# Two transformer layers on one core: when row maxima are turned, where counts run, and where scratch lies in the operand stage

## The chip, the cores and the metric

The kernel runs as one program on one core of a Trainium2 chip. Time is the device time of one execution in microseconds (us). TensorE (PE) does the matmuls and transposes, VectorE (DVE), ScalarE (ACT) and GpSimd (POOL) do the rest, and SyncE (SP) issues most DMAs. Each engine works through its own queue in order; semaphores order the engines among each other. PE writes its results to PSUM, which POOL does not touch in this kernel; everything else lies in SBUF.

## The reference

`x` is 2048 tokens by 512 features in float32. Each layer adds two branches to `x`, both computed from the same layer norm `xn`.

```
xn = layernorm(x)
x  = x + linear_attention(xn) + routed_experts(xn)        # layer 0
xn = layernorm(x)
x  = x + L1_attn(xn) + L1_ffn(xn)                         # layer 1

L1_attn: q, k, v = split(xn @ w_qkv)       # 16 heads of 32
         q, k = rope(rmsnorm(q)), rope(rmsnorm(k))
         softmax(q k^T / sqrt(32)) over the 1024 tokens before each token, and itself
         out = (p @ v) @ w_out
L1_ffn:  scores = xn @ w_router; take the 256 tokens of the highest score, sorted by place
         a transformer block on these 256 tokens alone: 16 heads of 128, 8 key heads,
         rms norms, rope by place, causal softmax, gated MLP of width 2048
         the result goes back to those 256 rows, the other rows keep xn
```

## The kernel before, in words

The span has four stages: layer 0, then for layer 1 the operand stage, the FFN block and attention. The change touches the operand stage and the FFN block.

**Operand stage.** The loop over 16 token tiles of 128 (`NT`, `t`) makes the queries, keys and values of layer 1. `turned` loads a tile of `xn` and transposes it on PE (`tr`, L100); ACT copies the result to `xnt`. Three groups of four matmuls (`p`, L782, 128x512 each) follow for q, k and v. `normed_qk` squares q and k on ACT (`t1`, L641), takes the norm on DVE (`rr`, `qk`, L642 to L645) and applies the rope on POOL (L650 to L660), for the last tile on DVE. One tile later `turned_qk` transposes q and k on PE (`trqk`); ACT copies to `qT`, DVE to `kT`.

**Row maxima.** Attention later needs the maximum of each score row. `maxima(i, ...)` finds it for query tile `i` in *steps*: four score matmuls (`pa`, L515, one for each head of a group, each listed as two records), mask matmuls (L521, L523), then one DVE reduction (`mx`, L527) of the whole PSUM buffer. There is one such buffer of four banks (`ps_a`, `bufs=1`), so a step's matmuls wait for the reduction of the step before. After a tile's last step DVE makes `nm` and `parts` (L531 to L534), PE transposes `parts` (`tn`, L537) and ACT copies to `negT`. All of it is issued at once, so `tn` stands on PE's queue right behind the last step.

**Steps between other work.** `Steps.some` spends a rate: at each call it owes a share of a step and issues one when a whole one is owed, of tiles below a bound only. In the operand stage the rate is 0.85, with six calls per tile, for query tiles 0 to 9 (`EARLY`); `early.upto(EARLY)` issues what is left before the last `turned_qk`. Tiles 10 to 15 are a second `Steps` object, `late`, with a PSUM pool of its own in the FFN block and a rate of 0.38; `late.upto(NT)` closes it. A query tile has four to twelve steps, 144 in all.

**Routing.** `routing` is a generator; each `next(route)` (four per tile) issues one piece. The first four pieces transpose the score row to all partitions (`srow`, L698, copied by ACT). Then each of the 16 token tiles has two count pieces on DVE: how many scores are larger (L713, L718, whole rows) and how ties are broken (L725, L726). From the counts come the places (`pplace`, `pos`), which POOL uses to scatter token numbers to lists in DRAM (L753), to load them back and to gather the 256 rows (`xs`, L579).

**FFN block.** It begins with a norm and transposes of the gathered rows (`hn_a`, L838, `trh_a`, L841) and the first projection (`k2p`, L852), whose weights are loaded by SP (`k2w`). `late.some` is called between its matmuls.

**What sets the order.** The order of the code is not the order on the engines: a planner reorders the instructions of each engine by their dependencies, and the engine then works in that order. In the profile counts ran far ahead of the token tile in whose pieces they were written: all sixteen lie between 782 and 862 us. Buffers are tiles of pools, and a pool's buffer that is reused, or lies where a closed pool's buffers lay, waits for those.

Of the kernel before, what the change touches and what calls it, by code (L numbers as in the profile page):

```python
# [19 lines left out]
P = 128  # L20
T = 2048
# [17 lines left out]
def two_layer_kernel(ctx: ExitStack, tc: tile.TileContext, a: dict, out: bass.AP):  # L39
# [452 lines left out]
    parts = []  # L492
    for n in range(2):
        pn = const([P, NC, 4, HD], f"parts{n}", l1, BF16)
        G.memset(pn, 0.0)
        parts.append(pn)

    def maxima(i, wk, ps_a, ps_t, ttag):
# [5 lines left out]
        mx = wk.tile([P, NC, 4, 3], F32, tag="mx", name=f"mx_{i}")  # L504
# [25 lines left out]
        nm = wk.tile([P, NC, 4], F32, tag="nm", name=f"nm_{i}")  # L530
        V.tensor_reduce(nm, mx[:, :, :, :nch], AX.X, ALU.max, negate=True)  # L531
        pn = parts[i % 2]
        vcopy(pn[:, :, :, 0], nm)
        V.tensor_tensor(pn[:, :, :, 1], nm, pn[:, :, :, 0], ALU.subtract)  # L534
        tn = ps_t.tile([P, NC, P], BF16, tag=ttag, name=f"tn_{i}")
        for g in range(NC):
            PE.transpose(tn[:, g, :], pn[:, g].rearrange("p h d -> p (h d)"), ident_b)  # L537
        scopy(negT[:, :, i * P : (i + 1) * P], tn)

    class Steps:  # L540


        def __init__(self, tiles, rate, **kw):
            self.tiles, self.kw = list(tiles), kw
            self.steps, self.now, self.rate, self.owed = iter(()), -1, rate, 0.0
            self.busy = False
# [10 lines left out]
        def one(self, below=NT):  # L557
            while self.now < below:
                if next(self.steps, False) is not False:
                    return True  # L560
                self.busy = False
                if not self.tiles or self.tiles[0] >= below:
                    return False
                self.now, self.busy = self.tiles.pop(0), True
                self.steps = maxima(self.now, **self.kw)
            return False

        def left(self):
            return self.tiles or self.busy

        def upto(self, below):
            while self.one(below):
                pass

# [7 lines left out]
    EARLY = 10  # L582


    with ExitStack() as p4:
        w4 = p4.enter_context(tc.tile_pool(name="w4", bufs=1, side="right", reuse_waits="tile"))
        xq = p4.enter_context(tc.tile_pool(name="xq", bufs=3, side="right", reuse_waits="tile"))
        r5 = p4.enter_context(tc.tile_pool(name="r5", bufs=1, side="right", reuse_waits="tile"))
        wk = p4.enter_context(tc.tile_pool(name="wk4", bufs=2, side="right", reuse_waits="tile"))
        ps_a = p4.enter_context(tc.tile_pool(name="ps_a4", bufs=1, **tight))  # L590
# [35 lines left out]
        def turned(t):  # L626
# [4 lines left out]
            xnt = wk.tile([P, NC, P], F32, tag="xnt", name=f"xnt_{t}")  # L631
# [3 lines left out]
        def normed_qk(t, pp):  # L635

            qk = wk.tile([P, 2, HEADS, HD], F32, tag="qk", name=f"qk_{t}")
            t1 = wk.tile([P, 2, HEADS, HD], F32, tag="t1", name=f"t1_{t}", bufs=1)
            rr = wk.tile([P, 2, HEADS], F32, tag="rr", name=f"rr_{t}")
# [13 lines left out]
            t2 = wk.tile([P, 2, HEADS, HD], F32, tag="t2", name=f"t2_{t}", bufs=1)  # L653
# [16 lines left out]
        def routing():  # L670
# [22 lines left out]
            srow = const([P, T], "srow", r5)  # L693
# [15 lines left out]
            for t in range(NT):  # L709
                own = score[:, t : t + 1]  # L710
                j1 = wk.tile([P, T], F32, tag="j1", name=f"j1_{t}", bufs=1)
# [37 lines left out]
            for n in range(4):  # L749
                place = wk.tile([P, 2 * HEADS], mybir.dt.int32, tag="rr", name=f"place_{n}")  # L750
# [23 lines left out]
        early = Steps(range(EARLY), 0.85, wk=wk, ps_a=ps_a, ps_t=ps_t, ttag="tr")  # L774
        xnt, last_qk = turned(0), None
        for t in range(NT):
            pp = []
            for j in range(3):
                pj = ps.tile([P, D], F32, tag="pj", name=f"p{j}_{t}")
                for c in range(NC):  # L780
                    w = w_v[:, c, :] if j == 2 else w_qk[:, c, j * D : (j + 1) * D]
                    PE.matmul(pj, xnt[:, c, :], w, start=c == 0, stop=c == NC - 1)  # L782
                    if c == 1:
                        early.some(min(t if j == 2 else t - 1, EARLY))
                        next(route, None)
                pp.append(pj)
                if j < 2 and last_qk is not None:
                    turned_qk(t - 1, last_qk, j)
                if j == 2 and t < NT - 1:
                    xnt = turned(t + 1)  # L790
                early.some(min(t if j else t - 1, EARLY))
                if j == 1:
# [513 lines left out]
```

## Time and profile before

| | us |
|---|---|
| median of 3 runs | 1873.57 |
| lowest, highest | 1873.55, 1880.08 |
| profiled execution | 1869.43 |
| its span | 1867.7 |
| layer 0 | 0 to 762.7 |
| operand stage | 762.7 to 1150.7 (388.0) |
| FFN block | 1150.7 to 1462.9 (312.2) |
| attention | 1462.9 to 1867.7 (404.8) |

The stages are cut at PE's first matmul of each. The granted clock, a share of PE's full speed, is 0.97 over the whole span. The token tiles of the operand stage start, by their first transpose, at 762.7, 783.4, 806.2, 831.3, 859.4, 878.9, 898.6, 915.9, 936.6, 961.8, 982.3, 1005.4, 1037.8, 1059.6, 1080.2 and 1102.1; the last one's window runs to the first `k2p` at 1150.7.

A group of instructions is written as line, engine, operation and `output<-input`, with buffer numbers left out. A wait is written `A <- B`: A's engine was idle before A, and B's end released it. Idle time of an engine that is not the bottleneck costs nothing by itself.

### The profile page before, as it was taken

Reading aid. Unit: us, or ns where it says so; the run is one execution under the profiler, and the core shown is the slowest. Engines: PE = TensorE matmul, PEld = TensorE weight load, DVE = VectorE, ACT = ScalarE, POOL = GpSimd, SP = SyncE. Lnnn points to the kernel's source line nnn. Section 1 sums busy time; section 2 is a strip of 40 time slices with the busy share of each in tenths; the row PEclk is TensorE's granted clock in tenths of the full one; section 3 lists DMA queues with packets and bytes.
Section 4 is the critical chain, followed back from the end, with each engine's and each line's share of the span. In section 5 each row is a group of like instructions: output and inputs, shape, how many; then the busy total and the mean of one; then the engine's idle time right before and its main releaser. Section 6 shows DMA issues by size and latency. Waiting matters only on the chain. (4 is left out here: it accounts for less than half of the span.)

```text
span 1867.7 us, 20604 instructions
## 1 busy us (share of the span) xinstructions
PE 1740.5 (93%) x8120; PEld 767.4 (41%) x8120; DVE 1008.1 (54%) x1445; ACT 573.7 (31%) x923; POOL 497.2 (27%) x372
## 2 busy tenths in 40 slices
PE   7999999999999999868988887999999999999999
PEld 4555444344444333323433333454565333333333
DVE  6775645436445343696666564575555455444344
ACT  3212334233233243111111111142100366446463
POOL 2110000100100110333344431331000467458583
PEclk9999999999999999989999897999999899999999
DMA  9301001210213130100001004311132300110100
GB/s 362 128 29 43 23 28 39 85 34 29 72 53 74 33 109 23 62 23 23 23 23 29 26 12 149 122 51 68 46 111 92 91 1 1 35 57 1 46 1 35
DMA packets 61810, 107.12 MB, mean 57 GB/s; under 512 B 12209, under 2 KB 13745, under 8 KB 61201
## 3 DMA queue, kind: packets, MB, share of 16 engines
q1 hardware_dynamic: 55280, 104.01, 16.7%
q0 software_dynamic: 1152, 1.21, 0.4%
q8 instruction: 63, 1.03, 0.2%
q10 hardware_dynamic: 5280, 0.59, 0.2%
q14 instruction: 35, 0.28, 0.0%
HBM read 84.14 MB, written 21.65 MB: 57 GB/s over the span
## 5 line engine op out<-in xcount | busy, mean ns | idle before, releaser
L527 DVE TENSOR_REDUCE mx<-pa 128x4 f32<-128x1536 f32 (+3 forms) x144 | 252.9, 1756 | 178.2 <-PE pa L523 83.8
L1210 POOL TENSOR_TENSOR acc<-acc,pt 128x1024 f32<-128x1024 f32 (+3 forms) x126 | 253.8, 2047 | 122.1 <-ACT pt L1137 75.8
L1137 ACT ACTIVATE pt<-ps 128x1024 f32<-128x1024 f32 (+3 forms) x208 | 182.2, 923 | 138.1 <-DVE ps L1128 86.4
L515 PE MATMUL pa<-kT,qT 32*128 32x384 f32 (+3 forms) x1152 | 158.0, 562 | 47.5 <-DVE mx L527 39.3
L1104 PE MATMUL ps<-qT,kT 32*128 32x512 f32 (+3 forms) x1152 | 162.0, 535 | 8.6 <-ACT pt L1137 8.1
L93 POOL TENSOR_TENSOR xr<-xr,xn 128x512 f32<-128x512 f32 x16 | 27.0, 1697 | 493.6 <-DVE xn L87 493.6
L424 PE MATMUL acc<-h,rw2T 128*128 128x512 f32 x256 | 135.3, 616 | 14.9 <-DVE h L290 14.3
L288 ACT ACTIVATE r_e<-eg 128x512 f32<-128x512 f32 x128 | 75.8, 594 | 222.4 <-PE eg L419 202.4
L782 PE MATMUL p<-w_qk,xnt 128*128 128x512 f32 x256 | 129.7, 631 | 8.3 <-ACT xnt L107 8.3
L290 DVE TENSOR_TENSOR h<-ea,r_e 128x512 f32<-128x512 f32 x128 | 87.0, 686 | 87.2 <-ACT r_e L289 59.9
L421 PE MATMUL ea<-xw,rw1T 128*128 128x512 f32 x256 | 130.7, 592 | 0.0
L419 PE MATMUL eg<-xl,rwgT 128*128 128x512 f32 x256 | 130.7, 592 | 0.0
L1128 DVE TENSOR_TENSOR ps<-ps,maskT 128x256 f32<-128x256 f32 (+1 forms) x144 | 68.3, 514 | 100.3 <-PE ps L1111 97.2
L1104 PEld LDWEIGHTS ps<-qT,kT 32*128 32x128 f32 x1152 | 62.2, 186 | 116.5 <-issue 55.4
L515 PEld LDWEIGHTS pa<-kT,qT 32*128 32x128 f32 x1152 | 52.0, 191 | 138.3 <-DVE mx L527 88.0
L1177 PE MATMUL av<-pt,v 128*32 128x512 f32 (+3 forms) x1024 | 102.3, 485 | 0.2
L415 DVE TENSOR_TENSOR xw<-xw,xl 128x512 f32<-128x512 f32 x64 | 43.9, 685 | 94.9 <-DMA xw<-w_d 94.9
L1219 DVE RECIPROCAL sm<-sm 128x128 f32<-128x128 f32 x64 | 61.8, 965 | 57.4 <-PE sm L1191 56.0
L424 PEld LDWEIGHTS acc<-h,rw2T 128*128 128x128 f32 x256 | 43.4, 188 | 95.5 <-DVE h L290 79.4
L289 ACT ACTIVATE r_e<-r_e 128x512 f32<-128x512 f32 x128 | 80.2, 629 | 6.4 <-issue 1.9
L650 POOL TENSOR_TENSOR t<-qk,cosg 128x1024 f32<-128x1024 f32 x15 | 35.3, 2354 | 161.7 <-DVE qk L645 145.5
L421 PEld LDWEIGHTS ea<-xw,rw1T 128*128 128x128 f32 x256 | 48.6, 190 | 61.2 <-issue 60.8
(278 smaller groups left out, 2542.2 us busy)
## 6 DMA issues: line engine op xcount, KB each, us to landing
xw<-w_d SPq DMA_DIRECT2D x64, 256.0 KB, 3.2
x<-in_x SPq DMA_DIRECT2D x16, 256.0 KB, 4.3
res_d<-x SPq DMA_DIRECT2D x16, 256.0 KB, 2.3
xr<-res_d SPq DMA_DIRECT2D x16, 256.0 KB, 4.8
xn_d<-xn SPq DMA_DIRECT2D x16, 256.0 KB, 2.4
res_d<-xr SPq DMA_DIRECT2D x16, 256.0 KB, 2.0
xnq<-xn_d SPq DMA_DIRECT2D x16, 256.0 KB, 2.9
v_d<-vt SPq DMA_DIRECT2D x16, 256.0 KB, 2.9
```

Of the source, the lines that this page charges most:

```text
L289: S.activation(r, r, AF.Square)
L290: V.tensor_tensor(dst, pa, r, ALU.mult)
L419: PE.matmul(pg, rwgT[:, e, hb], xl, start=True, stop=True)
L421: PE.matmul(pa, rw1T[:, e, hb], xw, start=True, stop=True)
L424: PE.matmul(acc, rw2T[:, j, e, :], h, start=e == 0 and j == 0, stop=e == E - 1 and j == 1,)
L515: PE.matmul(pS[:, h, : w * P], qT[r, g, i * P : (i + 1) * P], kT[r, g, ks], start=True, stop=not (edge or last),)
L527: V.tensor_reduce(mx[:, g, :, c], pS[:, :, : w * P], AX.X, ALU.max)
L782: PE.matmul(pj, xnt[:, c, :], w, start=c == 0, stop=c == NC - 1)
L1104: PE.matmul(pS[h // 2][:, h % 2, t0 * P - q0 : (t1 + 1) * P - q0], kT[r, g, kb * P : (kb + 1) * P], qT[r, g, t0 * P : (t1 + 1) * P], start ...
L1137: S.activation(pT[:, :, :n], pS[hp][:, :, :n], AF.Exp)
L1177: PE.matmul(self.av[h * HD : (h + 1) * HD, t0 * P - o : (t1 + 1) * P - o], vs[kb // 4][:, kb % 4, hs], got[h // 2][:, h % 2, t0 * P - q0 : ...
L1210: eng.tensor_tensor(part, part, got[hp][:, :, : q1 - q0], ALU.add)
```

## The change

The turn of a tile's maxima (`tn` and its copy) is no longer part of the tile's last step: `maxima` hands it out, and `Steps.one` issues it after the next step's matmuls. `mx` and `nm` become pairs of fixed buffers. `early` and `late` become one object with one PSUM pool over both stages; the limit `EARLY` goes, so in the operand stage steps of any finished tile are issued at rate 0.85 and no block of steps is issued at its end but three single ones around the last two `turned_qk`. What is left goes to the FFN block at a rate worked out from the number left over 190.

In the loop, the next tile's `xn` is transposed after the first of the three matmul groups rather than the third, and the previous tile's q and k after the second and third rather than the first and second. Some steps are allowed one call later (bound `t - 1` within the groups, `t` only at the third one's end). The routing starts at token tile 1. Each pair of counts first copies its two score columns into a buffer that rotates with `xnt`, so that it can't be issued far ahead of its tile. Scratch pools are split: `t1`, `rr`, `t2` and `place` lie in a pool `wka`, `srow` and `j1` in a pool `r6`, so that other buffers than before lie over those of layer 0.

The diff, without its empty lines:

```diff
@@ -489,19 +489,21 @@
-    parts = []
+    parts, mxs, nms = [], [], []
     for n in range(2):
         pn = const([P, NC, 4, HD], f"parts{n}", l1, BF16)
         G.memset(pn, 0.0)
         parts.append(pn)
-    def maxima(i, wk, ps_a, ps_t, ttag):
+        mxs.append(const([P, NC, 4, 3], f"mx{n}", l1))
+        nms.append(const([P, NC, 4], f"nm{n}", l1))
+    def maxima(i, ps_a):
         nb = min(i + 1, NWB)
         kb0 = i + 1 - nb
         nch = -(-nb // 4)
-        mx = wk.tile([P, NC, 4, 3], F32, tag="mx", name=f"mx_{i}")
+        mx, nm, pn = mxs[i % 2], nms[i % 2], parts[i % 2]
         for g in range(NC):
             lo = 0
             for c in range(nch):
@@ -527,23 +529,29 @@
                 V.tensor_reduce(mx[:, g, :, c], pS[:, :, : w * P], AX.X, ALU.max)
                 yield
                 lo += w
-        nm = wk.tile([P, NC, 4], F32, tag="nm", name=f"nm_{i}")
         V.tensor_reduce(nm, mx[:, :, :, :nch], AX.X, ALU.max, negate=True)
-        pn = parts[i % 2]
         vcopy(pn[:, :, :, 0], nm)
         V.tensor_tensor(pn[:, :, :, 1], nm, pn[:, :, :, 0], ALU.subtract)
-        tn = ps_t.tile([P, NC, P], BF16, tag=ttag, name=f"tn_{i}")
-        for g in range(NC):
-            PE.transpose(tn[:, g, :], pn[:, g].rearrange("p h d -> p (h d)"), ident_b)
-        scopy(negT[:, :, i * P : (i + 1) * P], tn)
+        def turn(pool, tag):
+            tn = pool.tile([P, NC, P], BF16, tag=tag, name=f"tn_{i}")
+            for g in range(NC):
+                PE.transpose(tn[:, g, :], pn[:, g].rearrange("p h d -> p (h d)"), ident_b)
+            scopy(negT[:, :, i * P : (i + 1) * P], tn)
+        yield turn
     class Steps:
-        def __init__(self, tiles, rate, **kw):
-            self.tiles, self.kw = list(tiles), kw
-            self.steps, self.now, self.rate, self.owed = iter(()), -1, rate, 0.0
-            self.busy = False
+        def __init__(self, ps_a):
+            self.ps_a, self.pool, self.tag, self.rate = ps_a, None, None, 0.0
+            self.steps, self.now, self.owed, self.done, self.turn = iter(()), -1, 0.0, 0, None
+        def place(self, pool, tag, rate):
+            self.pool, self.tag, self.rate = pool, tag, rate
         def some(self, below=NT, weight=1.0):
@@ -556,21 +564,30 @@
         def one(self, below=NT):
             while self.now < below:
-                if next(self.steps, False) is not False:
+                step = next(self.steps, False)
+                if step is None:
+                    self.done += 1
+                    self.turned()
                     return True
-                self.busy = False
-                if not self.tiles or self.tiles[0] >= below:
+                if step is not False:
+                    self.turned()
+                    self.turn = step
+                elif self.now + 1 >= below:
                     return False
-                self.now, self.busy = self.tiles.pop(0), True
-                self.steps = maxima(self.now, **self.kw)
+                else:
+                    self.now += 1
+                    self.steps = maxima(self.now, self.ps_a)
             return False
-        def left(self):
-            return self.tiles or self.busy
-        def upto(self, below):
-            while self.one(below):
+        def turned(self):
+            if self.turn is not None:
+                self.turn(self.pool, self.tag)
+                self.turn = None
+        def rest(self):
+            while self.one():
                 pass
+            self.turned()
     def rows_of(j):
         return bass.IndirectOffsetOnAxis(ap=idx[:, j : j + 1], axis=0)
@@ -579,15 +596,20 @@
         G.indirect_dma_start(out=dst, out_offset=None, in_=src[:, :], in_offset=rows_of(j))
     tight = dict(space=PSUM, reuse_waits="tile")
-    EARLY = 10
+    NSTEPS = sum(NC * -(-min(i + 1, NWB) // 4) for i in range(NT))
+    pa_in = ExitStack()
+    ps_a = pa_in.enter_context(tc.tile_pool(name="ps_a", bufs=1, **tight))
+    early = Steps(ps_a)
     with ExitStack() as p4:
         w4 = p4.enter_context(tc.tile_pool(name="w4", bufs=1, side="right", reuse_waits="tile"))
         xq = p4.enter_context(tc.tile_pool(name="xq", bufs=3, side="right", reuse_waits="tile"))
+        wka = p4.enter_context(tc.tile_pool(name="wka", bufs=2, side="right", reuse_waits="tile"))
         r5 = p4.enter_context(tc.tile_pool(name="r5", bufs=1, side="right", reuse_waits="tile"))
+        r6 = p4.enter_context(tc.tile_pool(name="r6", bufs=1, side="right", reuse_waits="tile"))
         wk = p4.enter_context(tc.tile_pool(name="wk4", bufs=2, side="right", reuse_waits="tile"))
-        ps_a = p4.enter_context(tc.tile_pool(name="ps_a4", bufs=1, **tight))
         ps = p4.enter_context(tc.tile_pool(name="ps4", bufs=3, **tight))
         ps_t = p4.enter_context(tc.tile_pool(name="ps_t4", bufs=1, **tight))
@@ -628,15 +650,15 @@
             xn = xnq.pop(t)
             if t + 2 < NT:
                 load_xn(t + 2)
-            xnt = wk.tile([P, NC, P], F32, tag="xnt", name=f"xnt_{t}")
+            xnt = wk.tile([P, NC, P], F32, tag="xnt", name=f"xnt_{t}", bufs=3)
             transpose4(ps_t, lambda c: xn[:, c * P : (c + 1) * P], xnt, f"tr2_{t}", scopy)
             return xnt
         def normed_qk(t, pp):
             qk = wk.tile([P, 2, HEADS, HD], F32, tag="qk", name=f"qk_{t}")
-            t1 = wk.tile([P, 2, HEADS, HD], F32, tag="t1", name=f"t1_{t}", bufs=1)
-            rr = wk.tile([P, 2, HEADS], F32, tag="rr", name=f"rr_{t}")
+            t1 = wka.tile([P, 2, HEADS, HD], F32, tag="t1", name=f"t1_{t}", bufs=1)
+            rr = wka.tile([P, 2, HEADS], F32, tag="rr", name=f"rr_{t}")
             for j in range(2):
                 S.activation(t1[:, j].rearrange("p h d -> p (h d)"), pp[j], AF.Square)
             V.tensor_reduce(rr, t1, AX.X, ALU.add)
@@ -650,7 +672,7 @@
             rope.tensor_tensor(
                 t1, qk, cosg[:, t].unsqueeze(2).to_broadcast([P, 2, HEADS, HD]), ALU.mult
             )
-            t2 = wk.tile([P, 2, HEADS, HD], F32, tag="t2", name=f"t2_{t}", bufs=1)
+            t2 = wka.tile([P, 2, HEADS, HD], F32, tag="t2", name=f"t2_{t}", bufs=1)
             for lo, s0 in ((0, HH), (HH, 0)):
                 rope.tensor_tensor(
                     t2[:, :, :, lo : lo + HH], qk[:, :, :, s0 : s0 + HH],
@@ -690,7 +712,7 @@
-            srow = const([P, T], "srow", r5)
+            srow = const([P, T], "srow", r6)
             for q in range(NT // 4):
                 tp = ps_t.tile([P, 4 * P], F32, tag="tr", name=f"srow_{q}")
                 for i in range(4):
@@ -707,8 +729,12 @@
             for n in range(4):
                 load(nc.sync, list_d[n][0:K2, :].rearrange("(j p) c -> p j c", p=P), lists[:, n])
             for t in range(NT):
-                own = score[:, t : t + 1]
-                j1 = wk.tile([P, T], F32, tag="j1", name=f"j1_{t}", bufs=1)
+                if t % 2 == 0:
+                    two = wk.tile([P, 2], F32, tag="xnt", name=f"own_{t}", bufs=3)
+                    vcopy(two, score[:, t : t + 2])
+                own = two[:, t % 2 : t % 2 + 1]
+                j1 = r6.tile([P, T], F32, tag="j1", name=f"j1_{t}")
                 if t > 0:
                     V.tensor_scalar(
                         j1[:, 0 : t * P], srow[:, 0 : t * P], own, None, ALU.is_ge, ALU.add,
@@ -747,7 +773,7 @@
             yield
             for n in range(4):
-                place = wk.tile([P, 2 * HEADS], mybir.dt.int32, tag="rr", name=f"place_{n}")
+                place = wka.tile([P, 2 * HEADS], mybir.dt.int32, tag="rr", name=f"place_{n}")
                 vcopy(place[:, 0:4], pos[:, 4 * n : 4 * n + 4, 0])
                 for i in range(4):
                     G.indirect_dma_start(
@@ -771,7 +797,7 @@
         route = routing()
-        early = Steps(range(EARLY), 0.85, wk=wk, ps_a=ps_a, ps_t=ps_t, ttag="tr")
+        early.place(ps_t, "tr", 0.85)
         xnt, last_qk = turned(0), None
         for t in range(NT):
             pp = []
@@ -781,23 +807,26 @@
                     w = w_v[:, c, :] if j == 2 else w_qk[:, c, j * D : (j + 1) * D]
                     PE.matmul(pj, xnt[:, c, :], w, start=c == 0, stop=c == NC - 1)
                     if c == 1:
-                        early.some(min(t if j == 2 else t - 1, EARLY))
-                        next(route, None)
+                        early.some(t - 1)
+                        if t > 0:
+                            next(route, None)
                 pp.append(pj)
-                if j < 2 and last_qk is not None:
-                    turned_qk(t - 1, last_qk, j)
-                if j == 2 and t < NT - 1:
-                    xnt = turned(t + 1)
-                early.some(min(t if j else t - 1, EARLY))
-                if j == 1:
+                if j == 0 and t < NT - 1:
+                    next_xnt = turned(t + 1)
+                elif j > 0 and last_qk is not None:
+                    turned_qk(t - 1, last_qk, j - 1)
+                early.some(t if j == 2 else t - 1)
+                if j == 1 and t > 0:
                     next(route, None)
+            xnt = next_xnt
             vt = wk.tile([P, D], F32, tag="vt", name=f"vt_{t}")
             scopy(vt, pp[2])
             load(nc.sync, v_d[t * P : (t + 1) * P, :], vt)
             last_qk = normed_qk(t, pp)
-        early.upto(EARLY)
+        early.one(NT - 1)
         for j in range(2):
             turned_qk(NT - 1, last_qk, j)
+            early.one(NT - 1)
         for _ in route:
             pass
@@ -808,11 +837,11 @@
         f5 = p5.enter_context(tc.tile_pool(name="f5", bufs=1, side="right", reuse_waits="tile"))
         fw = p5.enter_context(tc.tile_pool(name="fw", bufs=5, side="right", reuse_waits="tile"))
         wk = p5.enter_context(tc.tile_pool(name="wk6", bufs=2, side="right", reuse_waits="tile"))
-        ps_a = p5.enter_context(tc.tile_pool(name="ps_a6", bufs=1, **tight))
         ps = p5.enter_context(tc.tile_pool(name="ps6", bufs=4, **tight))
-        late = Steps(range(EARLY, NT), 0.38, wk=wk, ps_a=ps_a, ps_t=ps, ttag="mm")
+        late = early
+        late.place(ps, "mm", (NSTEPS - late.done) / 190.0)
         def stream(src, name):
@@ -1037,7 +1066,7 @@
                         start=f == 0, stop=f == INTER // P - 1,
                     )
                 late.some(weight=1.7)
-        late.upto(NT)
+        late.rest()
         gate = wk.tile([P, 2], F32, tag="sg", name="gate")
         S.activation(gate, listed[:, :, 1], AF.Exp, scale=-1.0)
         V.tensor_scalar_add(gate, gate, 1.0)
@@ -1050,6 +1079,8 @@
                 out=res_d[:, :], out_offset=rows_of(j), in_=delta[:, j, :], in_offset=None,
                 compute_op=ALU.add,
             )
+    pa_in.close()
```

## The prediction

> **What bounds the kernel now.** I read the head of the page first: whose time is it?
>
> ```profile
> span 1867.7 us, 20604 instructions
> PE 1740.5 (93%) x8120; PEld 767.4 (41%) x8120; DVE 1008.1 (54%) x1445; ACT 573.7 (31%) x923; POOL 497.2 (27%) x372
> ```
>
> TensorE (PE) is busy for 93%, so time is won where PE is idle or runs at a lower clock. Next I cut the span by stage (columns: window, its length, busy time and count of PE, weight load, VectorE (DVE), ScalarE (ACT), GpSimd (POOL); granted clock; DMA share; GB/s). The rows are the operand stage, the FFN block and attention.
>
> ```profile
> 762.70:1150.70 388.00, 319.71 (x1434) 137.75 (x1433) 263.07 (x331) 60.74 (x117) 140.54 (x102) 0.90 0.11 33
> 1150.70:1462.90 312.20, 294.62 (x1497) 158.00 (x1495) 172.66 (x176) 57.13 (x154) 51.29 (x73) 0.98 0.26 89
> 1462.90:1867.70 404.80, 391.82 (x3276) 138.06 (x3276) 183.47 (x312) 220.91 (x257) 255.42 (x127) 0.97 0.10 31
> ```
>
> The operand stage has 388.0 − 319.7 = 68.3 us without PE work, and a clock of 0.90 on top. Its waits (total us, times, longest us), all on PE:
>
> ```profile
> PE pa L515 <- DVE mx L527: 35.5, 24, 2.6
> PE tn L537 <- DVE parts L534: 11.4, 5, 3.3
> PE p L782 <- ACT xnt L107: 8.3, 10, 2.2
> PE pa L515 <- DVE kT L104: 8.1, 2, 6.4
> PE srow L698 <- ACT srow L107: 3.9, 1, 3.9
> ```
>
> Half of it is score matmuls (`pa`) waiting for DVE to empty their only buffer (`mx`). Then I cut the stage at each token tile's first transpose. Six of the sixteen rows:
>
> ```profile
> 783.40:806.20 22.80, 15.49 (x61) 7.35 (x60) 22.45 (x46) 3.73 (x7) 5.18 (x5) 0.85 0.08 24
> ...
> 831.30:859.40 28.10, 21.67 (x92) 9.43 (x90) 21.93 (x42) 3.86 (x7) 9.71 (x6) 0.82 0.06 18
> ...
> 898.60:915.90 17.30, 17.00 (x86) 7.52 (x85) 10.90 (x11) 3.06 (x6) 6.67 (x5) 1.00 0.11 31
> ...
> 1005.40:1037.80 32.40, 24.34 (x105) 9.62 (x104) 19.52 (x15) 4.45 (x8) 18.91 (x16) 0.82 0.09 25
> ...
> 1059.60:1080.20 20.60, 17.93 (x92) 7.50 (x89) 12.07 (x10) 3.27 (x6) 9.17 (x6) 1.00 0.04 17
> ...
> 1102.10:1150.70 48.60, 36.02 (x162) 15.94 (x161) 27.99 (x29) 6.75 (x15) 5.85 (x4) 0.74 0.16 54
> ```
>
> A clean tile is 17 to 21 us (898.6, 1059.6). In the first counted tiles DVE is full (22.45 of 22.80). The tile at 1005.4 and the end stand out. In the end's timeline (start, us, group, [idle before]):
>
> ```profile
> 1124.43 0.93 PE L515 MATMUL pa<-kT,qT 32*128 32x384 f32 x8 [2.61 <-DVE mx L527]
> ...
> 1127.54 1.66 PE L515 MATMUL pa<-kT,qT 32*128 32x384 f32 x8 [1.85 <-DVE mx L527]
> 1131.09 1.66 PE L515 MATMUL pa<-kT,qT 32*128 32x384 f32 x8 [1.88 <-DVE mx L527]
> ```
>
> Step after step with nothing between: PE waits out each `mx`, and the mean record of the same eight goes from 0.93 to 1.66 us as the clock falls.
>
> **The change part by part** (differences in us, against the profiled execution's 1869.43).
>
> *Tile 0 (20.7).* The routing starts a tile later, so four sets of `srow` transposes and the wait of 3.9 for their copies leave. That copy stood behind this on ACT:
>
> ```profile
> 776.25 0.60 ACT L641 ACTIVATE t<-p 128x512 f32<-128x512 f32 x1 [7.74 <-DMA res_d<-xr]
> ```
>
> The squares wait for layer 0's last store, since their scratch overlaps its buffers. In the new pools they don't; the late `srow` has that overlap, at a time when the store is done. Left: twelve pairs of `p` matmuls at 0.9 = 10.8, two transpose sets at 0.44, the first `xnt` wait, about 1: 13.6. **−7.**
>
> *Tile 1 (22.8).* Twelve pairs 10.8, the next `tr` 0.44, two `trqk` sets 0.9, four `srow` sets 1.8, a wait for POOL's rope (7.2 us a tile, begun at tile 0's end) of about 2, for `kT` 1. No `pa` step is left in this tile, so none waits the 6.4 for a `kT` copy that stood behind counts on DVE. **17, −6.**
>
> *Tiles 2 to 8 (25.1, 28.1, 19.5, 19.7, 17.3, 20.7, 25.2: 155.6).* The counts ran ahead on DVE from 782 to 846, in front of `kT` and `mx`; copying the two score columns into a buffer that rotates with `xnt` holds a pair to its tile. A count took 3.05 (792.17 to 795.22), two a tile 6.1. Without counts DVE needs 13.2 a tile (mean of seven later tiles): 19.3, over PE's 17.3. DVE is therefore the bound here, at 7 × 19.3 = 135 at best. A count issued ahead of an `mx` holds the next `pa`, and with it every PE instruction behind: I add 2 a tile: 150. **−5.** The extra copies (0.2, eight of them) are in this. The copies' new wait is for the slot of an older `xnt`; its readers are `p` matmuls of an earlier tile, long done. Were it late, the next `kT` and `mx` would stand behind it, and PE behind them.
>
> *A rule against it.* POOL's rope runs 7.2 of some 20 us here. In the trace the two-input counts (`L725`, `L726`) took 0.35 alone, and 0.79 to 1.64 in eight or so cases. The Trainium skill (GPSIMD Engine Reference, 1. Specifications) states that POOL shares SBUF interfaces with DVE, with contention for DVE instructions of two SBUF inputs. All 32 fell in 65 us before and lost about 4; spread over seven tiles with a rope in each, 11 of 32 (7.2/20) by 1.2 are an estimated 13, so 9 more: −36 for the whole instead of −45. The copies `p` → `xnt`, `mx` have one input and aren't touched by it.
>
> *Tiles 9 to 14 (140.3).* The tile at 1059.6, five steps at full clock, is the model: 20.6. Turning `tn` behind the next step's matmuls takes away the waits of 11.4; `xnt` transposed a matmul group earlier takes 0.7 a tile; the last `tn` wait, the one behind a `parts` that took 3.1 us at 1032.11 (0.23 elsewhere) while POOL issued list loads and ran a rope, has a step's matmuls in front of it. 6 × 20.6 = 124, with 1 for disorder 125. **−15.** POOL does the same work, the placing one tile later; its gathers ended at 1045, 100 us ahead of their reader (`hn_a`, 1145), and one tile later leave some 75. SP's queue is unchanged but for the loads of `xn`, issued two matmul groups earlier, with nothing but `v` stores beside them. `mx` and `nm` as two constants, and one score buffer for both stages instead of two pools, add no instruction; and the first FFN step no longer waits for a pool to be freed.
>
> *The end (48.6).* Before, `trqk` of tile 15 stood behind six steps at half clock; after, three steps lie between. Left: one tile 20.6; norm and rope on DVE with one `mx` between, about 7 (1119.51 to 1125.5); then the weight load `k2w`, which in both kernels waits for the last `trqk` (its buffer lies over `qk`): 1142.6 to 1150.7 = 8.1. **36, −12.5.** This is the floor; filling it with steps costs nothing.
>
> *FFN block.* About five more steps arrive (1.1 for matmuls and masks, 0.13 of switching): +6. Its `tn` waits, 4.1, go; some of 17.6 idle (POOL's ropes, 5.5) is filled: **0**, between −4 and +8 (five full `mx` waits at 1.8). Attention's order is the same: 0.
>
> Sum: −7 − 6 − 5 − 15 − 12.5 = −45.5. I take 5 of the contention estimate's 9: **−40**, so 1829 in the profile; the median of the runs is 1873.57, 4.1 above the profiled one, so **1834**.
>
> *A rule on the clock.* The last 48.6 us had 0.74 although no wait exceeded 2.6, and 806–831 kept 1.00 with waits up to 3.3. The skill (TensorE: Matmul & The Clock Gate, HAM oscillation) counts only PE idle gaps over about 3.4 us. By the rule alone the end would keep its half clock for another cause and only idle time would be won there: about 7 rather than 12.5, −35 in all. I go with the row: it fell within a run of waits at every step.
>
> **The rivals.**
> *The counts only move (1853).* DVE stays full in counted tiles: they lose the 11 gained in tiles 1 to 8 and pay contention of 9: −40 + 20 = −20. For: 19.3 against 17.3 leaves no slack. Against: tiles of 22 us or less hold it.
> *The end doesn't shrink (1846).* Steps again pace the turn of tile 15: −12 lost. For: they are still interleaved there. Against: three, not six.
> *No net change.* Break-even: without tiles 1 to 8 the gain is 34.5; over eight tiles (178.4 before) that is 26.6 us a tile. Between 25.4 and 27.8 it is within 9.4 us, the 0.5% that a measurement here can tell from no change.
> *Slower (1886).* In-order stalls: every counted tile becomes like 831.3, 28.1 long, with waits that halve the clock. 8 × 28.1 = 224.8, +46 − 34.5 = +12. For: that row exists with just such a mix. Against: it had five counts, not two.
>
> **How the numbers follow.** Main case with its variants (end not shrunk, gain 25 to 58) 0.70; counts moved, gain 10 to 25, 0.15; within 9.4 us 0.08; slower 0.05; more than 58 gained 0.02. Faster 0.87, same 0.08, slower 0.05. The range goes from −58 (1815: FFN idle filled, clock full) to −11.5 (1862), beyond which 0.15 is left. The main case's own range is 1815 to 1849.
>
> **What would show it.** First row of each tile: 13–15 for tile 0; 20 to 22 for tiles 2–8 with DVE over 85% and clock near 1; about 21 for 9–14, no `tn` wait; 36 for the end, clock over 0.85. `pa` waiting for `mx` falls from 35.5 to about 20. FFN block 308 to 320. Wrong if counted tiles pass 25 us, if a long `kT` wait returns, or if FFN takes over 325.

## The result, and the profile after

The changed kernel takes 1852.34 us (median of 7 runs, 1849.02 to 1862.40) against 1873.55 us before (7 runs, 1869.35 to 1880.08): a ratio of 0.9899, 95% interval 0.9879 to 0.9920. It is faster by 21 us. The prediction said 1834, 40 us faster, in a range of 1815 to 1862: the direction holds and the time lies in the range, but the gain is only about half of the one forecast. The profiled execution took 1849.02 us with a span of 1847.3, 20.4 less than before; the working below divides those 20.4.

The head of the page, kernel after:

```profile
span 1847.3 us, 20641 instructions
PE 1729.7 (94%) x8120; PEld 768.0 (42%) x8120; DVE 1021.2 (55%) x1453; ACT 573.7 (31%) x923; POOL 497.8 (27%) x372
```

The windows of the three stages of layer 1, kernel after (columns as before: window, length, busy time and count of PE, weight load, DVE, ACT, POOL, clock, DMA share, GB/s). The first row is the operand stage, cut from the first `tr` to the first `k2p`, then the FFN block and attention:

```profile
761.65:1117.78 356.13, 297.54 (x1377) 132.78 (x1376) 265.83 (x331) 59.97 (x116) 141.31 (x102) 0.92 0.10 34
1117.78:1437.04 319.26, 301.85 (x1557) 161.56 (x1557) 182.39 (x184) 57.72 (x155) 50.56 (x73) 0.97 0.26 88
1437.04:1847.30 410.26, 396.32 (x3274) 140.07 (x3272) 184.49 (x313) 221.19 (x257) 255.98 (x128) 0.96 0.10 31
```

The operand stage lost 31.7 us of its 387.8 (before, cut in the same way), the FFN block grew by 6.5 and attention by 5.9; layer 0 ended 1 earlier. Sum: −20.4.

The waits of PE in the operand stage, kernel after (total us, times, longest):

```profile
PE pa L517 <- DVE mx L529: 37.2, 17, 3.7
PE tn L539 <- DVE parts L534: 13.4, 5, 7.5
PE srow L720 <- ACT xnt L107: 2.8, 1, 2.8
PE p L808 <- ACT xnt L107: 2.2, 1, 2.2
...
PE pa L517 <- DVE kT L104: 0.5, 1, 0.5
```

The waits for `xnt` (8.3 before) and for `kT` (8.1) are much shorter. Those that were to shrink most are still there: `mx` 37.2 after 35.5 (forecast: about 20), and `tn` 13.4 after 11.4, with one wait of 7.5.

Since `tr` has moved, the tiles are compared here from each tile's first `p` matmul to the next one's (us, both kernels cut alike):

| tiles | before | after | difference | predicted |
|---|---|---|---|---|
| 0 | 19.3 | 12.8 | −6.5 | −7 |
| 1 | 22.7 | 16.6 | −6.1 | −6 |
| 2 to 8 | 156.0 | 156.6 | +0.6 | −5 |
| 9 to 14 | 140.5 | 133.5 | −7.0 | −15 |
| 15 and the end | 46.5 | 33.8 | −12.7 | −12.5 |
| FFN block | 312.8 | 319.3 | +6.5 | 0 |
| attention | 404.4 | 410.3 | +5.9 | 0 |

Some of the differences come with steps that moved: tile 1 holds none after one, tiles 2 to 8 hold 31 `mx` reductions after 32, tiles 9 to 14 hold 29 after 31, the end 8 after 9, and the FFN block five more.

Windows of six tiles after (1, 3, 6, 12, 13 and the last with the end):

```profile
777.26:793.85 16.59, 13.77 (x52) 7.11 (x53) 8.78 (x10) 4.96 (x10) 8.26 (x5) 1.00 0.09 33
...
814.38:835.62 21.24, 17.58 (x91) 8.60 (x90) 16.19 (x28) 3.75 (x8) 9.08 (x5) 0.92 0.08 25
...
880.97:905.04 24.07, 19.78 (x102) 8.70 (x101) 19.84 (x30) 4.10 (x8) 10.06 (x7) 0.93 0.08 22
...
1013.28:1043.94 30.66, 20.89 (x90) 8.81 (x89) 21.63 (x14) 3.38 (x7) 19.25 (x20) 0.78 0.06 18
1043.94:1064.83 20.89, 19.10 (x107) 8.36 (x105) 13.45 (x12) 3.74 (x7) 6.98 (x7) 1.00 0.11 32
1083.99:1117.78 33.79, 27.79 (x144) 13.03 (x141) 23.99 (x25) 6.26 (x14) 3.21 (x2) 0.82 0.16 49
```

Counted tiles (3, 6) are 21 to 24 us long at a clock of 0.92 to 0.93, neither PE nor DVE full. Tile 12 is 10 us longer than its neighbour. The end is short, as forecast; its clock is 0.82 after 0.73 (forecast: over 0.85).

Tile 12 from close by: DVE's rows, then POOL's, then PE's (start, us, group, [idle before]):

```profile
1029.29 0.19 DVE L532 TENSOR_REDUCE nm<-mx 128x16 f32<-128x32 f32 x1
1029.51 5.57 DVE L104 CAST parts<-nm 128x16 bf16<-128x16 f32 x1
1035.12 3.13 DVE L534 TENSOR_TENSOR parts<-nm,parts 128x16 bf16<-128x16 f32 x1
...
1029.13 0.97 POOL L779 DMA_INDIRECT list_d<-tokc,place  x1 [0.30 <-issue]
1030.13 2.40 POOL L672 TENSOR_TENSOR t<-qk,cosg 128x1024 f32<-128x1024 f32 x1
1032.50 2.52 POOL L677 TENSOR_TENSOR t<-qk,sing 128x512 f32<-128x512 f32 x2
...
1035.79 2.36 POOL L682 TENSOR_TENSOR qk<-t,t 128x1024 f32<-128x1024 f32 x1
...
1038.31 0.61 PE L539 MATMUL tn<-ident_b,parts 128*128 128x128 bf16 x4 [7.53 <-DVE parts L534]
```

Two operations on 16 numbers per partition, 0.2 us each in the median, take 8.7 us. The first begins while POOL issues a list store and ends at 1035.08, when POOL's third rope operation has just ended (1035.02); the second ends at 1038.25, when the last one has (1038.15). `tn` waits for them, and all of PE behind it.

### The profile page after: what moved, and what is told of

It is laid out like the page before. It is cut to its first block, busy times and chain, and to the rows that moved or that the text cites. A ratio compares the mean times of both kernels' runs of the same rounds, so it can differ in the third digit from the quotient of the medians.

```text
span 1847.3 us, 20641 instructions
## 1 busy us (share of the span) xinstructions
PE 1729.7 (94%) x8120; PEld 768.0 (42%) x8120; DVE 1021.2 (55%) x1453; ACT 573.7 (31%) x923; POOL 497.8 (27%) x372
## 4 chain that ended last, share of the span: by engine, by line
PE 43%; DVE 11%; ACT 2%; POOL 1%; issue 1%; DMA 0%; DVEq 0%; ACTq 0%
PE ps L1135 7%; PE pa L517 6%; PE p L808 5%; PE av L1208 5%; DVE mx L529 4%; PE po L1178 3%; PE sm L1222 2%; PE mg L1049 2%; PE pm L1064 1%; PE ps L1142 1%; PE mu L1053 1%; PE pao L1014 1%; DVE j L739 1%; PE pa L525 1%; PE q2p L881 1%
## 5 line engine op out<-in xcount | busy, mean ns | idle before, releaser
L517 PE MATMUL pa<-kT,qT 32*128 32x384 f32 (+3 forms) x1152 | 146.3, 561 | 45.3 <-DVE mx L529 44.5
L419 PEld LDWEIGHTS eg<-xl,rwgT 128*128 128x128 f32 x256 | 48.6, 190 | 61.2 <-issue 59.8
```

What stands on the lines that cost most here:

```text
L419: PE.matmul(pg, rwgT[:, e, hb], xl, start=True, stop=True)
L517: PE.matmul(pS[:, h, : w * P], qT[r, g, i * P : (i + 1) * P], kT[r, g, ks], start=True, stop=not (edge or last),)
```

## The experiments

All are compared with a run of the kernel before on the same chip; ratios are to that. For the changed kernel the ratio is 0.9899.

**1. Where the stall of tile 12 comes from.** The rope of that tile moves to DVE.

```diff
-            rope = V if t == NT - 1 else G
+            rope = V if t in (12, NT - 1) else G
```

> The changed kernel with the rope of token tile 12 on DVE instead of POOL (3.7 us more on DVE in that tile). Theory A, the 7.5 us that `tn` waits in tile 12 are POOL's ropes holding back the two tiny DVE operations on `parts` (5.57 and 3.13 us where they take 0.2): both are back near 0.2 to 0.8, the tile falls from 30.7 to about 23 us and the kernel by 8, to 1841 in the profile. Rival, the stall is DVE's own queue running late: `parts` still takes long or `tn` still waits over 4, the tile stays at 29 to 34 and the kernel at 1847 to 1853.

1847.66 us, 0.985 (0.981 to 0.989). In tile 12 the two operations are back at 0.19 and 0.22 us, and the tile fell from 30.7 to 25.4 (forecast: about 23). Tile 6, with the same instructions, grew from 24.1 to 28.1: there POOL now caught the two operations on `parts` (2.17 and 2.41 us), and the kernel stayed at 1847, where 1841 was forecast. The theory holds for its tile, but the stall depends on how POOL and DVE happen to meet, so moving one meeting makes another. This needed a test that takes the operations away instead.

**2. One operation instead of three.**

```diff
-        V.tensor_reduce(nm, mx[:, :, :, :nch], AX.X, ALU.max, negate=True)
-        vcopy(pn[:, :, :, 0], nm)
-        V.tensor_tensor(pn[:, :, :, 1], nm, pn[:, :, :, 0], ALU.subtract)
+        V.tensor_reduce(pn[:, :, :, 0], mx[:, :, :, :nch], AX.X, ALU.max, negate=True)
```

> The changed kernel with the tile's maxima written by one DVE reduction straight to the high bf16 half of `parts`; the copy and the subtraction behind it are left out (the low half stays zero; it shifts all scores of a row alike, numerator and denominator). Theory A, POOL's ropes hold back just those two operations: the 7.5 us wait of `tn` in token tile 12 and the smaller ones go, tile 12 falls from 30.7 to 21 to 24 us, `tn` waits in the operand stage from 13.4 to under 5, and the kernel by 8 to 12, to about 1839 in the profile. Rival, the reduction before them is late itself or is held back in their place: `tn` still waits over 10 in sum and the kernel stays within 4 us of the changed one.

1837.61 us, 0.9817 (0.9796 to 0.9837): 15 us under the changed kernel. Tile 12 took 21.4, tiles 9 to 14 took 122.4 (predicted for the change itself: 125). The waits of PE in its operand stage:

```profile
PE pa L517 <- DVE mx L529: 37.7, 19, 3.6
...
PE tn L537 <- DVE parts L532: 1.1, 1, 1.1
```

The view of the `parts` operations (count, then shortest, median and longest in ns), first of the changed kernel in the operand stage:

```profile
L104 DVE CAST parts<-nm x10: 194/210/5574, 811.0 to 1129.4; 128x16 bf16<-128x16 f32 x10
L534 DVE TENSOR_TENSOR parts<-nm,parts x10: 223/230/3129, 811.3 to 1129.7; 128x16 bf16<-128x16 f32 x10
```

and of this experiment, over all 16 tiles:

```profile
L532 DVE TENSOR_REDUCE parts<-mx x16: 164/219/230, 812.4 to 1423.4; 128x16 bf16<-128x48 f32 x8, 128x16 bf16<-128x16 f32 x4, 128x16 bf16<-128x32 f32 x4
```

The reduction is never held back (longest 230 ns), the copy and the subtraction are, up to 5574. `tn` waits of 13.4 became 1.1, and the operand stage fell by as much, from 356.1 to 344.1. The `mx` waits stayed (37.7 after 37.2).

**3. The same in the kernel before.** The same edit to the kernel before.

> The kernel before with one DVE reduction straight to `parts`, the copy and the subtraction left out. If the waits of `tn` (11.4 in the operand stage, 4.1 in the FFN block and at its end) came mainly of these two operations and POOL's hold on them: `tn` waits under 6 in the operand stage, 6 to 14 us faster than before. Rival, they came of the turn standing right behind the last step: `tn` waits of 8 or more stay, within 5 us of before.

1862.11 us, 0.9935 (0.9909 to 0.9961): 10.5 us, with `tn` waits in the operand stage of 3.4 after 11.4. The kernel before had this loss as well: time above each operation's shortest, summed over the `parts` rows of the operand stage, is 6.3 us before, 15.5 in the changed kernel, 0.1 here. So in the changed kernel these operations met POOL more often, by 9 us of DVE.

**4. What the counts cost, and whether their place matters.** The counts read the score column itself, free to run ahead:

```diff
-                if t % 2 == 0:
-                    two = wk.tile([P, 2], F32, tag="xnt", name=f"own_{t}", bufs=3)
-                    vcopy(two, score[:, t : t + 2])
-                own = two[:, t % 2 : t % 2 + 1]
+                own = score[:, t : t + 1]
```

> The changed kernel with the counts reading the score column itself, so that they may run ahead of their token tile again. Prediction's theory, spreading them saves: tiles 1 to 3 become long again (25 to 28 us each), 4 to 8 short (about 19), 5 us slower or more in tiles 2 to 8. Rival, the counts' work is only moved: tiles 2 to 8 sum to 150 to 160 us as now (156.6), the kernel within 4 us.

1846.24 us, 0.9869 (0.9826 to 0.9912), if anything faster than with the tie. Tiles 2 to 8 took 25.4, 27.2, 27.6, 20.2, 20.5, 18.8 and 18.4: 158.1 in sum against 156.6. Bunched or spread, they cost the same within the noise: the tie is worth nothing here.

Without any counts (only the yields stay):

> The changed kernel with all 32 count pieces left out, so the list of chosen tokens is that of the first 256 tokens: this prices the counts where they lie. If DVE is the bound of tiles 2 to 8, these fall from 156.6 to 125 to 135 us and the kernel by 22 to 30, to about 1822. Rival, the single score buffer sets these tiles: they stay above 147 and the kernel above 1838.

1825.47 us, 0.9767 (0.972 to 0.9814). Tiles 2 to 8: 125.6, 31 less. The operand stage of this experiment:

```profile
763.17:1091.23 328.06, 283.74 (x1377) 126.24 (x1376) 211.34 (x211) 59.45 (x116) 141.87 (x102) 0.96 0.14 47
```

DVE is busy 54.5 us less, the stage is 28 us shorter: in the mean over half of each count lies on the path. Where the 31 us lie, tiles 2 to 8 tell, first with the counts (changed kernel), then without them, each with PE's waits for `mx`:

```profile
793.85:950.49 156.64, 131.44 (x626) 59.57 (x625) 126.78 (x198) 25.38 (x48) 52.74 (x30) 0.91 0.08 24
PE pa L517 <- DVE mx L529: 21.4, 8, 3.7
...
796.95:922.55 125.60, 118.30 (x626) 53.58 (x625) 78.48 (x82) 24.73 (x48) 52.36 (x30) 1.00 0.10 32
PE pa L517 <- DVE mx L529: 2.7, 3, 1.5
```

PE has the same 626 instructions in both. With the counts it waits 19 us longer for `mx`, and its own instructions take 13 us longer, at a clock of 0.91 instead of 1.00.

**5. Counts on another engine.** The two long passes of each count run on ACT.

```diff
-                    V.tensor_scalar(
-                        j1[:, 0 : t * P], srow[:, 0 : t * P], own, None, ALU.is_ge, ALU.add,
-                        accum_out=cnt[:, t, 0:1],
-                    )
+                    S.activation(
+                        j1[:, 0 : t * P], srow[:, 0 : t * P], AF.Sign, bias=own, scale=-1.0,
+                        accum_out=cnt[:, t, 0:1],
+                    )
...
+            V.tensor_scalar(sel, sel, -0.5, 0.5 * (T - P), ALU.mult, ALU.add)
```

> The changed kernel with the two long passes of each count on ACT (sum of signs; equal scores in other token tiles would count half) instead of DVE, which takes some 36 us of work off DVE in tiles 2 to 8. Theory, DVE is the bound of these tiles: they fall from 156.6 to 130 to 140 us, the kernel to about 1827. Rival, ACT's passes of up to 2 us stand in front of its copies of `xnt`, `qT` and the squares: new waits for ACT of over 10 us in sum, and the tiles stay above 148.

1836.03 us, 0.981 (0.9775 to 0.9844): 16 us under the changed kernel. Tiles 2 to 8 took 141.5. This is short of the 130 to 140 expected, since tile 6 is 26.8, with a `tn` wait of 4.4 behind `parts` operations of 2.2 and 2.4; no new wait of PE for ACT appeared, though ACT took on some 34 us of work. So DVE's load is the cause of the long counted tiles; PE's waits for `mx` in them fell from 21.4 to 10.0.

**6. Both together** (experiments 2 and 5).

> The changed kernel with both: the long passes of the counts on ACT, and one reduction straight to `parts`. If DVE's load in token tiles 2 to 8 and the two held-back operations are separate causes, the gains of the two alone (15 and 16 us against the changed kernel) nearly add: 1818 to 1826. If they are the same time found twice, no better than the best of the two: 1833 to 1838.

1820.06 us, 0.9702 (0.9663 to 0.9742), 53 us faster than before: the gains add, so they are separate causes. Tiles 2 to 8 take 133.0, 9 to 14 take 120.1. Its operand stage and attention:

```profile
761.13:1081.79 320.66, 286.83 (x1377) 127.36 (x1376) 210.26 (x255) 93.58 (x176) 142.09 (x102) 0.95 0.11 37
...
1403.20:1818.60 415.40, 401.44 (x3274) 139.94 (x3272) 183.98 (x315) 221.11 (x257) 256.02 (x128) 0.94 0.10 30
```

**7. The turn.** The changed kernel with the turn issued at once:

```diff
-                    self.turned()
-                    self.turn = step
+                    step(self.pool, self.tag)
```

> The changed kernel with the turn of a tile's maxima issued at once, as before the change. Prediction's theory, the later turn was to save the 11.4 us of `tn` waits: 6 to 11 us slower, with `tn` waits of about 20 in the operand stage. Rival, a later turn saves nothing because DVE reaches `parts` no earlier than the next step's matmuls end: within 3 us of the changed kernel, `tn` waits 11 to 16.

1870.01 us, 0.9994 (0.998 to 1.0008): all of the gain is gone. But `tn` waits are not longer (10.6 in the operand stage). The FFN block takes 336.9, 17.6 more than in the changed kernel, and 24 more than before (it holds three more steps than in the changed kernel). Tiles 2 to 8 also grew, by 9, but the operand stage as a whole, with three steps fewer, by only 4. The FFN block's first tenth, by windows, and PE's timeline in it:

```profile
1124.00:1157.60 33.60, 24.20 (x105) 9.44 (x104) 15.74 (x14) 0.58 (x1) 4.13 (x6) 0.64 0.38 137
```

```profile
1131.78 1.66 PE L517 MATMUL pa<-kT,qT 32*128 32x384 f32 x8 [1.88 <-DVE mx L529]
...
1135.84 1.66 PE L517 MATMUL pa<-kT,qT 32*128 32x384 f32 x8 [1.85 <-DVE mx L529]
...
1139.89 1.66 PE L517 MATMUL pa<-kT,qT 32*128 32x384 f32 x8 [1.85 <-DVE mx L529]
1143.44 1.66 PE L517 MATMUL pa<-kT,qT 32*128 32x384 f32 x8 [1.88 <-DVE mx L529]
```

That is the picture of the end of the operand stage before: steps with nothing between them, 3.6 to 4.1 us each, and a mean clock of 0.64 over the window. The planner has put the run behind the first `k2p`.

The turn at once with the one reduction of experiment 2:

> The changed kernel with one reduction straight to `parts` and the turn issued at once. If the 20 us lost by turning at once came of the waits of `tn`, little of them is left with one short operation: within 5 us of the one reduction alone (1837). If they came of where the planner then puts the steps (a run of bare steps at the start of the FFN block, at 0.64 clock), the loss stays as long as that run stays: 1850 to 1860 with an FFN block over 330 us.

1847.32 us, 0.986 (0.9825 to 0.9894). `tn` waits are 2.0, and still it is 10 us behind the one reduction alone, with an FFN block of 336.2. The second reading holds in that the loss stays with the run of steps; the time is 3 us below what it named; the operand stage, with three steps fewer, took 339.0 instead of 344.1. So what undoing the turn costs is mainly where the steps end up. Why the planner places them there with the turn at once, no run shows.

The turn alone, on the kernel before (its `Steps` object keeps the turn and issues it after the next step):

> The kernel before with one part of the change alone: a tile's maxima are turned behind the next step's matmuls. If undoing this part cost 20 us because of its own waits, doing it alone gains 12 to 20 (1848 to 1858 in the profile). If the waits of 11.4 and 4.1 are all, it gains 5 to 12. If the loss on undoing came from where the planner then puts the steps between the two stages, doing it alone gives within 5 us of before.

1860.46 us, 0.994 (0.9919 to 0.996): 12 us, at the border of the first and the second reading; the interval, some 7 to 15 us, leaves both and excludes the third. `tn` waits fell from 11.4 to 4.4, its operand stage from 387.8 to 378.3. The end is 46.5, unchanged.

**8. Pools and routing alone**, on the kernel before (`t1`, `t2`, `rr` and `place` in a pool `wka`, `srow` and `j1` in `r6`; `next(route)` from tile 1):

> The kernel before with two parts of the change alone: scratch placed off layer 0's buffers, and routing started at token tile 1. By the prediction's sum tile 0 falls from 19.3 to about 13.5 and tile 1 by some 4 to 6: 8 to 12 us faster than before, 1858 to 1862 in the profile. Rival, the idle time only moves to the next tiles, whose counts start later: tiles 2 to 4 grow by as much, within 4 us of before.

1887.48 us, 1.0091 (1.0066 to 1.0116): slower. Tile 0 fell to 12.9, as forecast, tile 1 stayed at 22.9, and tiles 2 to 8 rose to 170.5 and 9 to 14 to 147.2. PE's waits in its operand stage, the first two (before: 35.5 for `mx`, 0.7 for `qk`):

```profile
PE pa L515 <- DVE mx L527: 43.7, 24, 3.5
PE trqk L100 <- POOL qk L662: 10.4, 2, 6.6
```

The 6 us of tile 0 are paid back by the counts, which now begin a tile later and lie in tiles 1 to 4 (26.7, 32.2 and 24.0 for tiles 2 to 4, after 25.1, 28.1 and 19.6), and twice `trqk` stands waiting for POOL's rope, 3.9 us in tile 1 and 6.6 in tile 13, the latter behind POOL's list stores and loads. So the 12.6 us of tiles 0 and 1 are no gain by themselves; the rest of the change offsets the return. The later `trqk`, which would take the waits for POOL, was not tried alone, nor was the earlier `xnt` or the one `Steps` object for both stages, so how the 21 us divide among the parts of the change is not shown.

**9. Steps moved back.** The rate in the operand stage is 0.95 instead of 0.85.

> The changed kernel with the rate of the steps in the operand stage at 0.95 instead of 0.85: some 5 to 8 more steps there and as many fewer in the FFN block. If a step costs the same at either place (1.3 to 1.6 us), the FFN block falls by 7 to 12 from 319.3, the operand stage rises by as much, and the kernel stays within 4 us. If the operand stage has idle time to hide them in, as the prediction assumed of the FFN block, the kernel gains 5 or more. If DVE is full there, it loses 5 or more, in tiles 2 to 8.

1842.27 us, 0.9843 (0.9807 to 0.988), 10 under the changed kernel, but not for the reasons given. Some seven steps moved (79 PE records): the FFN block fell by 15 to 304.3, and the end, where six of the seven went, rose by 20 to 53.9; `mx` is waited for eight times there, mostly in a run of bare steps. That alone would be a loss of 5. The gain is tile 12, 20.3 long: with other steps around it `parts` missed POOL's ropes (longest copy 0.9 us); attention was 4 shorter as well, which lies within its spread. So this run tells that a step more in the end costs over 3 us (20 for six, where the FFN block gave back 2 for each), not that the operand stage has room.

## Why the gain was half of the forecast

Three terms of the sum failed. Tiles 2 to 8 were priced by DVE's work and a small stall, and the stall was twice as long. In tiles 9 to 14 POOL's hold on `parts` was taken for covered, and it was not. In the FFN block five more steps were set off against waits that stayed. The terms for tiles 0 and 1 and for the end came out.

*Tiles 0 and 1 (−7, −6): right*, at −6.5 and −6.1. (The terms listed for tile 0 add to 12.7, not to 13.6; it took 12.8.) That this part stands for itself was wrong: alone it makes the kernel slower (experiment 8).

*The end (−12.5): right*, at −12.7, with a clock of 0.82 where over 0.85 was forecast. "Filling it with steps costs nothing" was not tested as such; 20 us for six steps in experiment 9 speak against it.

*Tiles 2 to 8 (−5): wrong, +0.6.* The step that failed is "holds a pair to its tile … 19.3 … DVE is therefore the bound here … I add 2 a tile". DVE's work was not too small in the sum: it is 18.1 a tile (126.8 over seven), with nearly all sixteen counts in these tiles, the five or six that tiles 0 and 1 had held before among them. But DVE alone, busy for 81%, doesn't set the tile's length: a tile takes 22.4, so DVE idles 4.3 of it, where the sum put 2. Through the one score buffer PE and DVE take turns; PE waits 21.4 us for `mx` in these tiles, 2.7 without counts, and the clock, forecast near 1, is 0.91 with the counts and 1.00 without. The view that spreading helps falls with the free counts of experiment 4; the cost itself (31 us for the counts) and its cause (DVE's load) are shown by 4 to 6.

*Tiles 9 to 14 (−15): −7.0, of which two steps fewer are a part.* "The last `tn` wait … has a step's matmuls in front of it" failed: one step's matmuls cover 1.3 us, and POOL held `parts` for 8.7. With that cause taken away these tiles reach 122.4 (experiment 2), where the sum had 125. The stall was in the profile before, in the row for `parts` at 1032.11, which ends with POOL's rope:

```profile
1032.11 3.12 DVE L534 TENSOR_TENSOR parts<-nm,parts 128x16 bf16<-128x16 f32 x1
...
1032.76 2.37 POOL L660 TENSOR_TENSOR qk<-t,t 128x1024 f32<-128x1024 f32 x1
```

I read it as a wait to be covered, not as one that could grow.

*The rule on shared interfaces* (the Trainium skill, GPSIMD Engine Reference, 1. Specifications) was put to the two-input counts, at 9 us more, and to nothing else. The counts, with the copies of their score columns, lost 7.3 us after against 4.6 before (each operation's time above the shortest of its shape, summed over tiles 1 to 15); the `parts` operations lost 15.5 against 6.3. So about 12 us of DVE were lost where 9 were priced, and the place was wrong: most fell where PE waits at once. I had taken operations of one input for safe. The row names DVE instructions in a 2-port perf mode beside those with two SBUF inputs, which my sum did not count, and the longest stall, 5.57 us, is that of a copy with one input; whether it ran in such a mode, no run here shows.

*FFN block (0): +6.5*, inside the stated −4 to +8, at its upper end. The difference is no noise: the seven kernels with these 76 reductions in the block have it between 318.1 and 321.4, the four built on the kernel before between 311.8 and 312.8. Five more steps came, as counted, and cost 6.7 of PE's busy time (301.85 − 295.13, some clock in it). The offsets didn't come: PE's time without work there is 17.4 after 17.6. Of the 4.1 of `tn` waits 2.1 went (1.3 inside the block; the 2.8 at attention's start became 2.0), and the waits for `mx` rose from 3.7 to 7.3.

*Attention (0): +5.9, and not from the change.* Its instructions are the same in all kernels here, and the fourteen profiles have it between 404.4 and 415.4 us, at clocks of 0.97 to 0.94: 404.4 to 412.4 in the four built on the kernel before, 406.5 to 415.4 in the others. The profile before was the lowest of all. A difference of 6 between two profiles of this stage can't be told from that spread, and the sum made against one profile carried that error unseen.

*The rule on the clock* (the Trainium skill, TensorE: Matmul & The Clock Gate, HAM oscillation): going with the row was right. In experiment 7 the mean clock was 0.64 around a stretch of six bare steps with no wait over 1.9 us. The end gained the 12.7 that the row gave, not the 7 of the rule alone: PE's idle time there fell by 6.1, its busy time, with one step fewer and the higher clock, by 6.6.

*The rivals.* "The counts only move" named the time (1853) and that tiles 2 to 8 gain nothing. That its total came out is luck in part: tile 1 kept its gain, DVE was not full, and the contention that it priced was real but hit `parts`. In the sum: tiles 2 to 8 missed by 5.6, tiles 9 to 14 by 8.0, the FFN block by 6.5, attention's spread by 5.9, and layer 0's earlier end and rounding give back about 1: 25 from −45.5 to −20.4. The 5 that I had taken for contention was the only allowance for any of it.

## What to carry to other kernels

A tiny operation between an engine that produces and one that waits is worth a look at its longest duration, not its mean: a copy and a subtraction of 0.2 us each were 8.7 us in one tile, and replacing them by an operation that POOL didn't hold back gave 15 us. Work that was spread differently on an engine that takes turns with PE cost the same; taking it to an idle engine gave 16. A block of steps that is moved past a stage's border is not gone: look for the run of bare steps on the other side, and sum both stages.

## What was not expected of the hardware

- DVE's copy to bf16 with one SBUF input (128x16) was held for 5.57 us, until the third of three rope operations on POOL had ended, and a copy of 128x2 f32 for 1.67; the two-input subtraction for 3.13. Reductions of the same size (0.16 to 0.23 us in 16 cases) and the long one-input count passes (1.28 us in the mean, 1.27 before) weren't stretched.
- With waits of 1.85 us in a row, each behind 1.7 to 2.3 us of matmuls, the mean granted clock was 0.64 over 33.6 us. The waits of up to 3.7 us that stand single in counted tiles left it at 0.85 to 0.93.
- One and the same instruction sequence (attention) took 404.4 to 415.4 us in different executions; the granted clock goes with it, from 0.97 to 0.94.
